# Another order of work in the head of an attention-and-MLP kernel, and two bias vectors computed on VectorE inside the MLP

## The chip, the cores and the metric

The kernel runs on one core of a Trainium2 chip. Its engines have one instruction queue each: TensorE (PE; its weight loads are listed as PEld), VectorE (DVE), ScalarE (ACT), GpSimd (POOL) and SyncE (SP), which here only issues DMAs. ACT and GpSimd issue DMAs as well, from the same queue as their computing instructions. Each engine goes through its queue in order, so an instruction that waits holds up all that stand behind it.

The metric is the device time of one execution in microseconds (us). Before the change it is 2689.59 us, the median of 3 runs (2689.32 to 2691.59).

## What is computed

Two layers on x of shape (2, 512, 32, 32), fp32. Layer 0 is attention with learned sampling positions and a position bias from a small network (its core is below), followed by an MLP. Layer 1 is full attention over the 1024 positions.

```python
# layer 0
xn  = bn(x)
q   = gconv1x1(xn, qw)                                  # 8 groups of 64 channels
off = gelu(depthwise_conv(q, off_dw_w, stride=4) + off_dw_b)
off = tanh(einsum('bchw,oc->bohw', off, off_pw_w)) * 4  # where the 64 keys are sampled
kv  = grid_sample(xn, grid + off)
k, v = gconv1x1(kv, kw), gconv1x1(kv, vw)
pos  = grid_q - grid_kv                                 # (query, key, 2)
bias = sign(pos) * log1p(abs(pos))
bias = relu(bias @ cpb_w1 + cpb_b1)                     # 2 -> 128
bias = relu(bias @ cpb_w2 + cpb_b2)                     # 128 -> 128
bias = bias @ cpb_w3 + cpb_b3                           # 128 -> 1, per query and key
attn = softmax(q k^T * scale + bias)
x = x + out_w (attn v) + out_b
x = x + mlp_w2 gelu(mlp_w1 bn2(x) + mlp_b1) + mlp_b2
# layer 1
q, k, v = x Wq^T + bq, x Wk^T + bk, x Wv^T + bv
x = x + (softmax(q k^T / sqrt(512)) v) Wp^T + bp
```

In layer 1 the kernel multiplies weight matrices with each other beforehand: G = Wq^T Wk for the logits, and the product of Wp and Wv for the output. The biases then shrink to two vectors of 512 numbers, Wk^T bq and Wp bv (+ bp). These two are the "two bias vectors" of the change.

## The kernel before

**Chains.** The 8 pairs of an image and a block of 128 channels (two groups of 64) are worked through in 5 chains: chain 0 and chain 1 with one pair each, chains 2 to 4 with two each. A chain (`chain(ci)`) makes the queries of its pairs (normalise, L260, on ACT; matmuls psq, L266; copies into qa, L271), the depthwise convolution (in chain 0 as 36 taps on VectorE, L303 and L305), gelu (L337), a small matmul po (L345), tanh (L355), and from the positions th the tile ab with sign(pos) * log1p(abs(pos)) for each of 32 coordinates and each key: ab = fe[:, 1], finished by L390. Then ab is written to a scratch tensor in DRAM, fdr, by four DMAs of SP (L392), one for each quarter c of the keys, in runs of 16 floats. `sample(ci)` after it makes the keys and values.

**Main loop.** 256 steps s, each for 4 keys of one group. `load_tables` (L592) loads, every 4 steps, the 16 keys' values back from fdr to all 128 partitions (fb, 512 KB, one buffer, on SP's queue); `st_tables` turns fb into ta (L602) and tb (L607 on VectorE for the first, L609 on ACT for the others). `st_layer1` (L621, VectorE) forms relu(ta + tb) for 4 keys and all queries, h1; `st_layer2` (L638) does 64 passes of TensorE into PSUM; ACT evicts them (L645, L647) into rx, ua or uo, and ub; VectorE adds pairs (L655); and GpSimd's and SP's DMAs add and move parts of the result (a fold, L669; a join, L672 on SP and L674 on GpSimd). A join of one step waits for the fold of the same step. L703 puts the result into the logits. The instructions of chains 1 to 4 are laid between those of the steps as a background program (`later`), one piece per step.

**The head** is everything before the loop's first step. `wake` runs matmuls on zeros (L147). All loads are issued on SP and ACT. `rank()` finds how many of the 128 hidden units have positive last weights and where each goes (two matmuls with one column, L212 and L213, small operations on GpSimd and six on VectorE, L219 to L225); `arrange()` puts the hidden units in that order with matmuls (L229, L232). `weights(0)` and `weights(1)` are the two products of weight matrices (psg, L524, 16 matmuls of two passes each; copied out by ACT, L529, and stored to gdr by GpSimd, L530). `vectors()` computes the two bias vectors with TensorE: 8 matmuls psu (L539), a copy, 8 matmuls put (L548), a copy into ub (L552), and the addition of bp on GpSimd (L553).

Several helpers set the order: `issue_after(x)` places what is recorded inside it behind instruction x in the order in which instructions are laid out; generators (`head`, `g`, `n`, `v`) are advanced by `next`, so that a piece of one is recorded between pieces of another. The tile pools decide by tags and numbers of buffers when a tile may be written again; an instruction that writes a tile waits for its last readers.

**After the loop** comes the projection of layer 0 (L884, L892), in two halves, then the MLP as 8 units (L937), each unit loading its weights on SP, then layer 1's attention (L1056, L1154).

Of the kernel before, what the change touches and what calls it, by code (L numbers as in the profile page):

```python
# [34 lines left out]
    ("bq", 4), ("bv", 4), ("bp", 4), ("dwb", 1), ("cb1", 1), ("cb3", 1),  # L35
# [11 lines left out]
def conv_seq_kernel(ctx: ExitStack, tc: tile.TileContext, x, xt, kst, pst, cst, vec, wsm, outw, w1, w2, wl, out):  # L47
# [16 lines left out]
    for i, g in enumerate(("bn1g", "bn2g")):  # L64
        nc.gpsimd.tensor_scalar(
            bns[:, 4 * i : 4 * i + 4], vs[:, VOFF[g] : VOFF[g] + 4], INV_BN, None, ALU.mult
        )
# [73 lines left out]
    with tc.tile_pool(name="lp", bufs=2) as lp:  # L141
# [20 lines left out]
        nc.gpsimd.memset(prod, 0.0)  # L162
# [12 lines left out]
        nc.scalar.dma_start(out=pz[:, 0:413], in_=pst)  # L175
        nc.scalar.dma_start(out=ws[:, 1024:1408], in_=wsm[:, 1536:1920])
        nc.scalar.dma_start(out=ident, in_=kst)
        nc.scalar.dma_start(out=cs, in_=cst)
# [7 lines left out]
        nc.scalar.dma_start(out=ws[:, P:1024], in_=wsm[:, P:1024])  # L186
# [20 lines left out]
        perm, place = pw_[:, 256:384], pw_[:, 384:512]  # L207
        def rank():
            nc.gpsimd.memset(one, 1.0)
            nc.gpsimd.tensor_scalar(po_, wb[:, 0:1], 0.0, None, ALU.is_ge)  # L210
            ps = flat("rank")
            nc.tensor.matmul(ps[:, 0:1], tri, po_, start=True, stop=True)  # L212
            nc.tensor.matmul(ps[:, 512:513], one, po_, start=True, stop=True)  # L213
            nc.scalar.copy(rn, ps.rearrange("p (h n) -> p h n", h=2)[:, :, 0])
            r_, n_ = rn[:, 0:1], rn[:, 1:2]
            nc.gpsimd.tensor_scalar(pc, chan, n_, r_, ALU.add, ALU.subtract)
            nc.gpsimd.tensor_scalar(dc, pc, r_, po_, ALU.subtract, ALU.mult)
            nc.gpsimd.tensor_tensor(pc, pc, dc, ALU.subtract)
            nc.vector.tensor_scalar(k16, four, n_, 4.0, ALU.is_le, ALU.mult)  # L219
            nc.vector.tensor_reduce(t4, k16, AX.X, ALU.add)  # L220
            free, bound = ([t.rearrange("p (a b l) -> p b a l", a=2, b=2)[:, i] for t in (place, crow)] for i in (0, 1))
            nc.vector.tensor_scalar(bound[0], bound[1], t4, 64.0, ALU.is_ge, ALU.mult)
            nc.vector.tensor_tensor(bound[0], bound[0], bound[1], ALU.add)
            nc.vector.tensor_scalar(free[0], free[1], t4, None, ALU.add)
            nc.vector.tensor_scalar(perm, place, pc, None, ALU.is_equal)  # L225

        def arrange():
            ps = flat("perm")
            nc.tensor.matmul(ps[:, 0:P], w2t, perm, start=True, stop=True)  # L229
            for z in range(4):  # L230
                for u in range(4):
                    nc.tensor.matmul(  # L232
                        ps[32 * u : 32 * u + 32, 512 + 2 * z : 514 + 2 * z], perm[:, 32 * z : 32 * z + 32], wb,
                        start=True, stop=True,
                    )
            nc.scalar.copy(cw2, ps[:, 0:P])
            nc.scalar.copy(
                sc[:, 0:8].rearrange("p (a z) -> p z a", a=2), ps[:, 512:520].rearrange("p (z a) -> p z a", a=2)
            )
            nc.gpsimd.tensor_scalar(sc[:, 8:9], sc[:, 1:2], 0.0, 2.0, ALU.is_ge, ALU.mult)  # L240
            nc.gpsimd.tensor_scalar(sc[:, 8:9], sc[:, 8:9], 1.0, None, ALU.subtract)
            nc.gpsimd.tensor_scalar(sc[:, 0:4], sc[:, 0:4], sc[:, 8:9], None, ALU.mult)
            for z in (1, 3):
                nc.gpsimd.tensor_tensor(sc[:, 4 + z : 5 + z], sc[:, 4 + z : 5 + z], sc[:, z : z + 1], ALU.mult)
            nc.gpsimd.tensor_scalar(w3f[:, 24:32], mask[:, 0:8], sc[:, 8:9], None, ALU.mult)
            nc.gpsimd.tensor_scalar(w3u[:, 28:32], mask[:, 8:12], sc[:, 8:9], None, ALU.mult)

# [3 lines left out]
        def chain(ci):  # L251
# [3 lines left out]
            for i in range(K):  # L255
# [14 lines left out]
                for f_, h_, f, h in QUADS:  # L270
                    nc.scalar.copy(  # L271
                        qa[f_, b, k, h * 512 : (h + 1) * 512], ps[h_, f * 512 : (f + 1) * 512]
                    )
# [67 lines left out]
            ps = flat("po")  # L341
            with tc.issue_after(marks[0]) if ci == 0 else nullcontext():
                for i in range(3):
                    for f in range(2):
                        nc.tensor.matmul(  # L345
                            ps[:, f * 512 + i * n // 2 : f * 512 + (i + 1) * n // 2],
# [7 lines left out]
            for f in range(2):  # L354
                nc.scalar.activation(  # L355
                    th.rearrange("p i (f k) j -> p f i (k j)", f=2)[:, f],
                    ps[:, f * 512 : f * 512 + 3 * n // 2].rearrange("p (i m) -> p i m", i=3), AF.Tanh,
                )
            if ci == 0:

                nc.scalar.activation(hb[:, 9:10], thf[:, 3 * n - 1 : 3 * n], AF.Ln, bias=1.0, scale=0.0)
            if ci > 0:
                yield
            for i in range(3):
                nc.vector.scalar_tensor_tensor(
                    th[:, i], th[:, i], 4.0, jg[:, i].unsqueeze(1).to_broadcast([P, 2 * K, J]),
                    ALU.mult, ALU.add,
                )
            nc.vector.tensor_scalar(thf, thf, 2.0 / 7.0, -1.0, ALU.mult, ALU.add)
# [15 lines left out]
            nc.vector.reciprocal(u, u)  # L385
            nc.vector.tensor_tensor(er, er, u, ALU.mult)
# [4 lines left out]
            for c in range(4):  # L391
                nc.sync.dma_start(  # L392
                    out=fdr[ci][:, c, :, :].rearrange("g p j -> p g j"),
                    in_=ab.rearrange("p (g c j) -> p g c j", c=4, j=KT)[:, :, c, :],
                )
# [111 lines left out]
        with tc.issue_after(nc.cur_bb.bb.instructions[-1]):  # L507
            nc.sync.dma_start(out=wv, in_=wsm[:, 1024:1536])
            nc.sync.dma_start(out=ow_s, in_=outw)
        gs = lp.tile([P, 2, NCH, C], F32, tag="h1", name="gs", bufs=3)  # L510
        bz = ph.tile([P, 2 * NCH, 32], F32, tag="xnt", name="bz")
        nc.gpsimd.memset(bz, 0.0)
        for i, bn in enumerate(("bq", "bv")):
            nc.gpsimd.tensor_copy(
                bz[:, i * NCH : (i + 1) * NCH, 0], vs[:, VOFF[bn] : VOFF[bn] + NCH]
            )

        def weights(i):
            ps = [flat("psg") for _ in range(2)]
            for o in range(NCH):  # L520
                if o == NCH - 1:
                    yield
                for k in range(NCH):
                    nc.tensor.matmul(  # L524
                        ps[k // 2][:, k % 2 * 512 : k % 2 * 512 + 512], wls[i][:, 0, o, k * P : (k + 1) * P],
                        wls[i][:, 1, o, :], start=(o == 0), stop=(o == NCH - 1),
                    )
            for k2 in range(2):
# [4 lines left out]

        def vectors():
            ps = flat("psu")
            rows = ph.tile([P, 2, C], F32, tag="wt", name="rows")
            for i in range(2):
                for o in range(NCH):
                    nc.tensor.matmul(  # L539
                        ps[32 * o : 32 * o + 32, 512 * i : 512 * i + 512], bz[:, i * NCH + o, :],  # L540
                        wls[i][:, 1, o, :], start=True, stop=True,
                    )
            nc.scalar.copy(rows.rearrange("p i c -> p (i c)"), ps)
            yield
            ps = flat("put")
            for i in range(2):
                for k in range(NCH):
                    nc.tensor.matmul(  # L548
                        ps[:, 512 * i + k : 512 * i + k + 1], rows[:, i, k * P : (k + 1) * P], ones,
                        start=True, stop=True,  # L550
                    )
            nc.scalar.copy(ub, ps.rearrange("p (i c) -> p i c", i=2)[:, :, 0:NCH])  # L552
            nc.gpsimd.tensor_tensor(  # L553
                ub[:, 1, :], ub[:, 1, :], vs[:, VOFF["bp"] : VOFF["bp"] + NCH], ALU.add
            )

        def newest(engine):
            return next(i for i in reversed(nc.cur_bb.bb.instructions) if i.engine == engine)

        marks = []  # L560
        head, g, n, v = chain(0), weights(0), weights(1), vectors()
        next(head)
        next(head)
        rank()
        next(head)
        next(g)
        marks.append(newest(mybir.EngineType.PE))
        next(head)

        with tc.issue_after(newest(mybir.EngineType.PE)):  # L570
            next(g, None)
        for _ in head:
            pass
        arrange()
        next(v)
        next(n)
        with tc.issue_after(newest(mybir.EngineType.PE)):
            next(v, None)
# [19 lines left out]
        def st_tables(c):  # L598
# [3 lines left out]
            nc.scalar.activation(  # L602
                ta.rearrange("p j x -> p x j"), fb[:, 0], AF.Identity, bias=col("cb1"), scale=col("w1x")
            )
# [234 lines left out]
    nc.gpsimd.tensor_tensor(uc, ub[:, 0, 0:2], ub[:, 0, 2:4], ALU.add)  # L839
# [16 lines left out]
    with ExitStack() as top, tc.tile_pool(name="wp", bufs=2) as wp:  # L856
# [171 lines left out]
        for i, (b, p) in enumerate(units):  # L1028
            if 0 < i < len(units) - 1:
                load_unit(*units[i + 1])  # L1030
# [5 lines left out]
            layer1(p, wa, xb, hm)  # L1036
            if p == NU - 1 and b == 0:
# [4 lines left out]
            if p == NU - 1 and b == 0:  # L1042
                spread([xb[:, j] for j in range(7)])

# [212 lines left out]
def _layout(np, inputs):  # L1257
# [7 lines left out]
    def twice(v):  # L1265
# [6 lines left out]
        "mb2": cols(L0["mlp_b2"]), "bq": cols(L1["bq"]), "bv": cols(L1["bv"]), "bp": cols(L1["bp"]),  # L1272
# [29 lines left out]
    def quarters(w):  # L1302
# [15 lines left out]
        "wl": wl,  # L1318
    }
# [20 lines left out]
```

## Time and profile before

| | |
|---|---|
| median of 3 runs | 2689.59 us |
| the profiled execution, whole | 2690.77 us |
| its span, first to last instruction | 2688.9 us |
| mean granted TensorE clock | 0.998 |
| TensorE busy | 2664.8 us, 99% |
| VectorE busy | 2244.6 us, 83% |
| ScalarE busy | 1689.0 us, 63% |
| GpSimd busy | 575.3 us, 21% |
| first loop step's matmuls start | 46.61 us |
| first matmul of the MLP starts | 1996.00 us |

A time in the profile is in us from the start of the span. A group's line reads: line, engine, operation, written and read tiles, shapes, how often; then busy time and the mean of one in ns; then the idle time of that engine just before these instructions, and what ended it. In a timeline a line gives the start, the length, and in brackets the idle time before it with what released it. In the chain of waits each piece is what the end depended on at that moment; "SPq" is time in which SP's queue was issuing. A granted clock of 0.50 means that TensorE ran at half speed.

### The profile page before, as it was taken

How to read it: one execution, taken by the hardware profiler on the slowest of the kernel's cores; microseconds unless marked ns; L12 is line 12 of the kernel's file. 1: busy time of each engine (PE TensorE's matmuls, PEld its weight loads, DVE VectorE, ACT ScalarE, POOL GpSimd, SP SyncE). 2: the span in 40 equal slices, each digit the busy share in tenths (PEclk: the TensorE clock that was granted, in tenths of full speed). 3: DMA queues.
4: the chain of work that ended last, by engine and by line, in shares of the span. 5: the costliest groups of instructions: out<-in, count | busy, mean ns of one | idle time of the engine just before them, and what ended most of it. 6: DMA issues, size and time to landing. Idle time of an engine off the chain costs nothing.

```text
span 2688.9 us, 46981 instructions
## 1 busy us (share of the span) xinstructions
PE 2664.8 (99%) x19628; PEld 955.2 (36%) x19628; DVE 2244.6 (83%) x1337; ACT 1689.0 (63%) x2191; POOL 575.3 (21%) x617
## 2 busy tenths in 40 slices
PE   9999999999999999999999999999999999999999
PEld 3323323232333323233333333333344444446455
DVE  5999999999999999999999999999765484466354
ACT  4787798789878788877777777777621131114041
POOL 1222222222222222222222222222243222000000
PEclk9999999999999999999999999999999999999999
DMA  5667776677666676666676776766631110000000
GB/s 186 146 147 148 154 148 138 139 159 154 141 148 144 150 149 145 139 147 142 148 155 138 148 151 145 147 149 142 134 122 47 47 47 32 16 16 0 31 1 31
DMA packets 95219, 314.05 MB, mean 117 GB/s; under 512 B 17184, under 2 KB 19872, under 8 KB 92320
## 3 DMA queue, kind: packets, MB, share of 16 engines
q0 software_dynamic: 57168, 201.88, 40.4%
q1 hardware_dynamic: 36832, 108.02, 11.2%
q8 instruction: 155, 2.54, 0.4%
q10 hardware_dynamic: 1008, 1.15, 0.1%
q14 instruction: 56, 0.46, 0.0%
HBM read 71.67 MB, written 6.55 MB: 29 GB/s over the span
## 4 chain that ended last, share of the span: by engine, by line
PE 85%; DVE 6%; issue 4%; ACT 2%; DMA 2%; SPq 0%; POOL 0%; DVEq 0%; POOLq 0%; ACTq 0%
PE ps L638 54%; PE sw L937 14%; PE sw L1056 9%; DVE h L621 3%; PE sw L1154 2%; PE sim L703 2%; PE psg L524 1%; PE sw L884 1%; DVE ub L655 1%; DMA ua<-uo 1%; DVE uo L655 1%; DMA ua<-ua 0%; ACT prod L313 0%; DVE ua L655 0%; ACT rx L645 0%
## 5 line engine op out<-in xcount | busy, mean ns | idle before, releaser
L638 PE MATMUL ps<-h,cw 128*32 128x512 f32 x16384 | 1786.6, 593 | 12.3 <-ACT rx L645 10.7
L621 DVE CUSTOM_DVE_ANT_1 h<-ta,tb 128x4096 f32<-128x4096 f32 (+1 forms) x257 | 1131.3, 4402 | 47.0 <-PE ps L638 42.0
L638 PEld LDWEIGHTS ps<-h,cw 128*32 128x32 f32 x16384 | 533.9, 110 | 1231.7 <-issue 1151.7
L645 ACT ACTIVATE rx<-ps,sc 128x1024 f32<-128x1024 f32 x512 | 568.3, 1110 | 175.0 <-PE ps L638 165.5
L647 ACT ACTIVATE ub<-ps,sc 128x1024 f32<-128x1024 f32 x256 | 308.0, 1203 | 96.4 <-PE ps L638 96.2
L655 DVE SCALAR_TENSOR_TENSOR ub<-rx,sc,ub 128x1024 f32<-128x1024 f32 x256 | 326.5, 1275 | 5.7 <-ACT ub L647 5.5
L657 POOL DMA_DIRECT2D ua<-ub x128 | 115.1, 899 | 723.6 <-DVE ub L655 692.3
L937 PE MATMUL sw<-xb,w1t 128*128 128x512 f32 x448 | 193.7, 592 | 1.3 <-DVE xs L123 1.3
L657 POOL DMA_DIRECT2D uo<-ub x127 | 119.3, 939 | 348.8 <-DVE ub L655 289.0
L937 PE MATMUL sw<-hm,w2t 128*128 128x512 f32 x448 | 193.6, 592 | 0.0
L647 ACT ACTIVATE ua<-ps,sc 128x1024 f32<-128x1024 f32 x128 | 154.1, 1204 | 58.5 <-PE ps L638 58.3
L674 POOL DMA_DIRECT2D ua<-uo x126 | 109.7, 870 | 365.2 <-DMA ua<-uo 355.5
L647 ACT ACTIVATE uo<-ps,sc 128x1024 f32<-128x1024 f32 x128 | 154.1, 1204 | 42.0 <-PE ps L638 38.8
L655 DVE SCALAR_TENSOR_TENSOR ua<-rx,sc,ua 128x1024 f32<-128x1024 f32 x128 | 163.5, 1277 | 12.5 <-ACT ua L647 12.5
L655 DVE SCALAR_TENSOR_TENSOR uo<-rx,sc,uo 128x1024 f32<-128x1024 f32 x128 | 163.5, 1277 | 11.8 <-ACT uo L647 11.8
L123 DVE TENSOR_TENSOR hm<-hm,sw 128x1024 f32<-128x1024 f32 x56 | 67.5, 1220 | 110.8 <-PE sw L937 110.6
L669 POOL DMA_DIRECT2D ua<-ua x126 | 154.8, 1229 | 2.6 <-DMA ua<-ub 1.5
L937 PEld LDWEIGHTS sw<-xb,w1t 128*128 128x128 f32 x448 | 85.1, 190 | 108.8 <-issue 105.0
L946 ACT ACTIVATE hm<-hm,vs 128x512 f32<-128x512 f32 x64 | 42.6, 714 | 129.0 <-DVE hm L123 129.0
L937 PEld LDWEIGHTS sw<-hm,w2t 128*128 128x128 f32 x448 | 85.2, 190 | 107.1 <-issue 106.4
L123 DVE TENSOR_TENSOR xs<-xs,sw 128x1024 f32<-128x1024 f32 (+1 forms) x48 | 55.5, 1170 | 72.2 <-PE sw L1056 36.0
L1056 PE MATMUL sw<-aT,vt 128*128 128x512 f32 x224 | 96.7, 593 | 0.3 <-ACT aT L1136 0.3
(237 smaller groups left out, 1798.7 us busy)
## 6 DMA issues: line engine op xcount, KB each, us to landing
ua<-ub POOLq DMA_DIRECT2D x128, 512.0 KB, 4.8
uo<-ub POOLq DMA_DIRECT2D x127, 512.0 KB, 5.4
fb<-fdr SPq DMA_DIRECT2D x64, 512.0 KB, 5.1
ua<-ua POOLq DMA_DIRECT2D x126, 256.0 KB, 6.4
ua<-uo SPq DMA_DIRECT2D x126, 256.0 KB, 2.8
ua<-uo POOLq DMA_DIRECT2D x126, 256.0 KB, 3.8
w1t<-in_w SPq DMA_DIRECT2D x8, 1024.0 KB, 4.8
w2t<-in_w SPq DMA_DIRECT2D x8, 1024.0 KB, 4.8
```

Of the source, the lines that this page charges most:

```text
L123: nc.vector.tensor_tensor(out, a, b_, op)
L621: nc.vector._custom_dve(TENSOR_ADD_SAT, out=h1[:, y : y + step].rearrange("p y t x -> p (y t x)"), in0=a.unsqueeze(1).to_broadcast([P, ste ...
L638: nc.tensor.matmul(ps[32 * q : 32 * q + 32, h, :], cw2[:, 32 * z : 32 * z + 32], h1[:, 16 * h : 16 * h + 16, q, :], start=True, stop=True,)
L645: nc.scalar.activation(o, ps, AF.Relu, bias=sc[:, 4 + z : 5 + z])
L647: nc.scalar.activation(o, ps, AF.Relu, bias=sc[:, 4 + z : 5 + z], scale=sc[:, z : z + 1])
L655: nc.vector.scalar_tensor_tensor(r[1], r[0], sc[:, z : z + 1], r[1], ALU.mult, ALU.add)
L657: nc.gpsimd.dma_start(out=sums[s][1], in_=sums[s][3], accum_op=ALU.add)
L669: nc.gpsimd.dma_start(out=lanes(s, 0), in_=lanes(s, 1), accum_op=ALU.add)
L674: nc.gpsimd.dma_start(out=lanes(s, 1), in_=lanes(s + 1, 0), accum_op=ALU.add)
L703: nc.tensor.matmul(sims[gi][q : q + 32, :], w_, t[:, h, :], start=(i == 0 and f == 0), stop=(i == NSL // 4 - 1 and m == len(parts[e]) - 1),)
L937: nc.tensor.matmul(ps[:, m, :], w[:, a, k, m * P : (m + 1) * P], x[:, b_, k, :], start=(k == 0), stop=(k == 1),)
L1056: nc.tensor.matmul(ps[:, m, :], w[:, a, k, c + m * P : c + (m + 1) * P], x[b_][:, k, :], start=(k == 0), stop=(k == nk - 1),)
```

## The change

1. Loads. cs, pz and ident are issued by GpSimd instead of ACT; the later part of ws by SP, behind the output weights, instead of ACT. The scales bns come from VectorE instead of GpSimd. The clearing of prod moves into `arrange()`.
2. Order of TensorE's work. Queries, then 4 products of `weights(0)`, the two ranking matmuls, 9 products, po, the last 3 products, the arranging matmuls, and the 16 products of `weights(1)`. The ranking, po and arranging matmuls of the head write tiles of the `sim` pool. Half of the first chain's copies into qa are done by VectorE.
3. Order of the small work. The VectorE part of the ranking (`order()`) stands behind the taps. The load of the logarithm's table does not read th. For chain 0 the part of th that ab needs is placed first, the rest after the write. The reciprocal writes a tile of its own. The first ta is made in two pieces.
4. The write of ab to fdr is one DMA instead of four, in all chains.
5. `vectors()` is removed. In each of the 8 MLP units SP loads a 128x512 piece of a matrix (wr; and br, one of the biases, spread over all partitions, at two of the units), and VectorE multiplies the two and sums along the row into one column of ub. The two additions that use ub come after the MLP's units.

```diff
-        nc.gpsimd.tensor_scalar(
+        nc.vector.tensor_scalar(
             bns[:, 4 * i : 4 * i + 4], vs[:, VOFF[g] : VOFF[g] + 4], INV_BN, None, ALU.mult
         )
...
-        nc.scalar.dma_start(out=pz[:, 0:413], in_=pst)
         nc.scalar.dma_start(out=ws[:, 1024:1408], in_=wsm[:, 1536:1920])
-        nc.scalar.dma_start(out=ident, in_=kst)
-        nc.scalar.dma_start(out=cs, in_=cst)
+        nc.gpsimd.dma_start(out=cs, in_=cst)
+        nc.gpsimd.dma_start(out=pz[:, 0:413], in_=pst)
+        nc.gpsimd.dma_start(out=ident, in_=kst)
...
-        nc.scalar.dma_start(out=ws[:, P:1024], in_=wsm[:, P:1024])
...
-                    nc.scalar.copy(
-                        qa[f_, b, k, h * 512 : (h + 1) * 512], ps[h_, f * 512 : (f + 1) * 512]
-                    )
+                    copy = nc.vector.tensor_copy if ci == 0 and h == 1 else nc.scalar.copy
+                    copy(qa[f_, b, k, h * 512 : (h + 1) * 512], ps[h_, f * 512 : (f + 1) * 512])
...
-                nc.scalar.activation(hb[:, 9:10], thf[:, 3 * n - 1 : 3 * n], AF.Ln, bias=1.0, scale=0.0)
+                with tc.issue_after(newest(mybir.EngineType.Activation)):
+                    nc.scalar.activation(hb[:, 9:10], ones, AF.Ln)
...
+            place_keys(2 if ci == 0 else 0, 3)
...
-            nc.vector.reciprocal(u, u)
-            nc.vector.tensor_tensor(er, er, u, ALU.mult)
+            rc = acc.rearrange("p a k y x -> p (a k y x)")[0:64, 0:n]
+            nc.vector.reciprocal(rc, u)
+            nc.vector.tensor_tensor(er, er, rc, ALU.mult)
...
-            for c in range(4):
-                nc.sync.dma_start(
-                    out=fdr[ci][:, c, :, :].rearrange("g p j -> p g j"),
-                    in_=ab.rearrange("p (g c j) -> p g c j", c=4, j=KT)[:, :, c, :],
-                )
+            nc.sync.dma_start(
+                out=fdr[ci].rearrange("g c p j -> p (g c) j"), in_=ab.rearrange("p (g j) -> p g j", j=KT)
+            )
+            if ci == 0:
+                place_keys(0, 2)
...
             nc.sync.dma_start(out=ow_s, in_=outw)
+            nc.sync.dma_start(out=ws[:, P:1024], in_=wsm[:, P:1024])
...
-        head, g, n, v = chain(0), weights(0), weights(1), vectors()
+        head, g, n = chain(0), weights(0), weights(1)
         next(head)
         next(head)
-        rank()
+        next(g)
+        with tc.issue_after(newest(PE)):
+            rank()
         next(head)
-        next(g)
-        marks.append(newest(mybir.EngineType.PE))
+        with tc.issue_after(newest(PE)):
+            next(g)
+        marks.append(newest(PE))
         next(head)
-
-        with tc.issue_after(newest(mybir.EngineType.PE)):
-            next(g, None)
+        with tc.issue_after(newest(PE)):
+            next(g)
+        order()
         for _ in head:
             pass
-        arrange()
-        next(v)
-        next(n)
-        with tc.issue_after(newest(mybir.EngineType.PE)):
-            next(v, None)
+        with tc.issue_after(newest(mybir.EngineType.Activation)):
+            next(g, None)
+        with tc.issue_after(newest(PE)):
+            arrange()
+        with tc.issue_after(newest(PE)):
+            next(n)
         next(n, None)
...
-            nc.scalar.activation(
-                ta.rearrange("p j x -> p x j"), fb[:, 0], AF.Identity, bias=col("cb1"), scale=col("w1x")
-            )
+            for j0, j1 in ((0, 4), (4, KT)) if c == 0 else ((0, KT),):
+                nc.scalar.activation(
+                    ta.rearrange("p j x -> p x j")[:, :, j0:j1], fb[:, 0, :, j0:j1], AF.Identity,
+                    bias=col("cb1"), scale=col("w1x"),
+                )
...
         for i, (b, p) in enumerate(units):
+
+            j, k = divmod(i, NCH)
+            if k == 0:
+                br = cp.tile([P, C], F32, tag="kz", name="br")
+                nc.sync.dma_start(out=br, in_=brow[j].partition_broadcast(P))
+            wr = f_pool.tile([P, C], F32, tag="ss", name="wr")
+            nc.sync.dma_start(out=wr, in_=wlt[:, i])
...
             layer1(p, wa, xb, hm)
+            nc.vector.scalar_tensor_tensor(
+                wr, wr, 1.0, br, ALU.mult, ALU.mult, accum_out=ub[:, j, k : k + 1]
+            )
```

## The prediction, made before the changed kernel was run

> **What bounds the kernel now.** The page first. TensorE is busy for the whole span at full granted clock, so outside the head only a hole in the row of matmuls can cost or give time.
>
> ```profile
> span 2688.9 us, 46981 instructions
> PE 2664.8 (99%) x19628; PEld 955.2 (36%) x19628; DVE 2244.6 (83%) x1337; ACT 1689.0 (63%) x2191; POOL 575.3 (21%) x617
> L638 PE MATMUL ps<-h,cw 128*32 128x512 f32 x16384 | 1786.6, 593 | 12.3 <-ACT rx L645 10.7
> ```
>
> Next the list of waits for PE (us in total, times, longest): the rows left out bring the sum to some 20 us. L212 and L266 are the head, L645 is a stall of the loop's evictions, L884 and L937 stand in and after the projection.
>
> ```profile
> PE ps L638 <- ACT rx L645: 10.7, 12, 3.0
> ...
> PE rank L212 <- POOL pwork L210: 1.5, 1, 1.5
> ...
> PE sw L937 <- DVE xs L123: 1.3, 1, 1.3
> PE sw L884 <- DVE xs L123: 1.2, 1, 1.2
> PE psq L266 <- ACT xn L260: 1.0, 1, 1.0
> ```
>
> Then the timeline of PE in the head (start, length), and one row of busy time by stretches (stretch, its length, the five engines' busy time, granted clock, DMA share, GB/s): from 9.45, inside the second hole, the clock is halved for 6.83 us.
>
> ```profile
> 7.56 1.09 PE L266 MATMUL psq<-xn,ws 64*64 64x512 f32 x8 [1.04 <-ACT xn L260]
> 10.17 0.59 PE L212 MATMUL rank<-pwork,pz 128*128 128x1 f32 x2 [1.53 <-POOL pwork L210]
> ...
> 30.89 10.57 PE L524 MATMUL psg<-wl_s 128*128 128x512 f32 x24
> ...
> 46.61 0.64 PE L638 MATMUL ps<-h,cw 128*32 128x512 f32 x4
> ```
>
> ```profile
> 9.45:16.28 6.83, 6.11 (x11) 3.04 (x11) 4.97 (x24) 3.04 (x5) 1.91 (x8) 0.50 1.05 416
> ```
>
> Last, the chain of waits around the largest hole of the loop, 503.47 to 506.47: ab's last operation (L390), four writes of fdr on SP's queue, a join (L672), the load of fb, then ACT's table, for which ACT had waited since 499.6 with evictions behind it.
>
> ```profile
> 492.61 0.42 DVE fe L390
> ...
> 493.04 0.63 SPq L392
> ...
> 497.27 1.77 SPq L392
> ...
> 499.27 0.51 SPq L672
> ...
> 499.89 3.74 DMA fb<-fdr
> ...
> 504.74 0.68 ACT tb L609
> ...
> 506.47 5.75 PE ps L638 x33
> ```
>
> **Head: TensorE's side.** Before, the first loop step starts at 46.61 and ends at 53.68 in the chain of waits. Three things go. (1) The holes of 1.04 and 1.53: xn (L260) started at 6.26, behind ACT's own issues at 4.70, 5.34 and 5.71; now ACT issues three loads early and the scales come from VectorE (vs landed at 4.68, two operations of some 0.2), so xn runs 5.0 to 6.25 under the wake matmuls, which end at 6.51. Queries follow to 7.6 and then four products, no rank: together 2.57. (2) Half clock: 6.11 us of busy time at 0.50 would take half as long, 3.05. (3) The 16 vector matmuls, 1.76 + 1.68 on the chain: 3.44. Sum 9.06. Laid out forwards, with 0.44 per pass (10.57 / 24): queries to 7.6, 8 passes to 11.1, rank 0.5, 18 passes to 19.6, po 0.85 to 20.5, 6 passes to 23.1, perm 0.7, 32 passes to about 37.9. The products' loads are no bound: the slice of each o is in by 6.50, 8.49, 11.90 and 13.26, before its turn.
>
> [...]
>
> **Head: the tables' side.** The taps start after four copies of 2.35 in all, 7.7 + 2.35 = 10.05 instead of 11.10. The copies are now split over ACT and DVE, but the built program's semaphores make each wait for the one before, so nothing is gained there. The six ranking operations (about 1.1 us between the taps) move behind them, so gelu ends near 19.0 and po waits for TensorE's 19.6. From po's end (20.5): tanh 0.6, table load 1.28, 0.15, then Abs at 22.55; Abs to the end of ab took 28.16 to 31.82, 3.66, less 0.85 because the reciprocal no longer waits for Ln to release its tile: 25.4 (before 31.82; the load used to hold the third L365 until 27.13, and two of the three now come later). Write: before, 31.85 to the load's issue at 37.04, 5.2, for the first of four writes; now one write of all 512 runs. Bounds: 4.4 (a little under the median 4.7 of the 20 single writes) and 7.7 (first issue to last landing of the four at chain 2). I take 5.2, as the bytes are few: 30.6. Load 3.33: 33.9. ta's first quarter about 0.5 (between 0.28 for a 128x64 operation and 1.27 for all), both halves of h1 4.5: 38.95. The first four matmuls of the step (8 passes, 1.75) cover 37.9 to 39.6, so this path is just hidden. Step 0 ends at 37.9 + 7.0 = 44.9: **-8.8**. At 4.4 and 0.428 a pass -9.4; at 7.7 h1 ends 41.45, the step 46.7: -7.0.
>
> At no price: the three loads on GpSimd's queue. Each issue takes about 0.9 (the L657 and L674 rows), so they go out by 4.7, and pz is first needed at 11.1; VectorE is idle until then, GpSimd has only memsets, and prod's (1.38) moves to a free stretch. The late part of ws (448 KB) sits behind the output weights on SP, ahead of xnt and xn of chain 1, which nobody waits for before the loop. ACT's gs copies go behind Ln; they only delay buffers needed at 23.
>
> **Loop: the chains' write.** In chains 1 to 4 four issues become one, and the first load must wait for all of it. At chain 2 that meets the stall shown. In the built order the last operation of ab stands behind the 4.41 of layer 1 on VectorE (before: ahead of it, 492.61), and the join of L672 stands ahead of the write on SP. That join waits for a GpSimd fold issued at 490.72 that landed at 497.52 (the page's median for it is 6.4). So the write goes at about 497.7, not 493.04; SP no longer spends 6.0 on four issues. Landing 4.5 to 7.7 (the four together took 7.7, 9.1 and 6.8 in chains 2 to 4), load 3.7: fb at 507.7 against 503.63, **+4.1**. What is late next: ACT's table, the eviction behind it (rx L645), then TensorE, whose PSUM is full. Here nothing else is in front of ACT, so all of it shows, plus 0.3 of half clock (the 3.0 stall was followed by 3.3 us at 0.52): **+4.4**. Lower bound 0.4 (fold lands at once, write as fast as one of the 20, 3 us), upper 8.0. Chains 1, 3 and 4 have their first tables requested later than the write lands in the trace; chain 4's hole (1.94, from sg's wait of 2.4 on the write) may shrink or stay: 0.
>
> **Projection and MLP.** Ten loads and eight VectorE operations on 128x512. Nearest row for one: L892, 0.74 (1.27 for 128x1024 bounds it above). In VectorE's order five of them stand inside the second projection, 1957 to 1996, where VectorE is nearly dense; its pauses there are 0.78 + 1.59 + 0.68 = 3.05. All share one buffer, so each load (256 KB, 2.9 from issue to landing for such a load at 1943.27) starts only when the previous operation is done: I count 1.8 and 0.3 of waits, with the queue behind them (the sums L123 and L892 that TensorE needs). 5 x 0.74 + 2.1 - 3.05 = **+2.7** on the start of the MLP; 0.65 if loads are in time, 5.8 if no pause is used. The other three sit in unit 0, where VectorE pauses some 2 us per product. The two GpSimd sums replace two and feed the last stage only.
>
> **Sum.** -8.8 + 4.4 + 2.7 = -1.7. The profiled execution took 2690.77 (span 2688.9 and 1.9 around it), 1.2 above the median shown: 2690.77 - 1.7 - 1.2 = **2687.9**.
>
> **Rivals.** (A) As summed, 0.50; own range 2684.4 to 2692. (B) The stall of chain 2 does not grow, because fold and write land fast, and the projection costs 1.7, half way between its lower bound and my value: -8.8 + 0.4 + 1.7 = -6.7, 2682.9, faster; 0.30. For it: single writes landed in as little as 2.1, and SP loses 6 us of issuing. Against: the chunks are the same and start later. (C) The write is late for every chain: first tables wait at chains 1, 3 and 4 as at 2, 4.4 each. -8.8 + 4 x 4.4 + 2.7 = +11.5, 2701; it decides from three chains on (+7.1, 2696.7). For it: the same code in all chains. Against: only two waits of ACT for fb stand in the trace, one of them the head's. 0.12. (D) The head gives half, because the clock stays low or the write takes 7.7 and more: -5 + 4.4 + 2.7, 2691.7; 0.08.
>
> **Numbers.** This kernel's runs tell about 0.2% (5.4 us) from no change: faster is under 2684.2, slower over 2695.0. Faster 0.32 (B, a little of A), same 0.54 (A, D), slower 0.14 (C, A's upper bounds). Range: -9.4 + 0.4 + 0.65 gives 2681.2 below; -7.0 + 8.0 + 5.8 would give 2696.4; cut to 2694.5.
>
> **To look for.** The head without a half-clock stretch and with the first L638 near 38; fdr written once, landing within 4.4 to 7.7; a PE hole of some 7 us near 494 to 502, with SP's write behind the join; VectorE's new operation waiting for wr before the MLP. Wrong if the loop's hole is 3 or less (B), if several chains show one (C), or if the head still shows clock 0.5 (D).

## The result, and the profile after

The changed kernel takes 2686.23 us (median of 20 runs, 2684.04 to 2688.40); the kernel before, run beside it, 2690.39 us (20 runs, 2688.26 to 2691.97). The ratio is 0.9987, with a 95% interval of 0.9981 to 0.9993: about 3.5 us faster by the ratio (4.2 between the medians), inside 0.2%. The profiled execution took 2687.88 us with a span of 2686.1 us, 2.8 less than the 2688.9 of before.

Line numbers from here on are those of the changed kernel: L629, L636, L612, L405, L726 and L727 were L638, L645, L621, L390, L735 and L736 before. The page's line for the busiest group, and the list of PE's waits (us in total, times, longest), of the changed kernel:

```profile
L629 PE MATMUL ps<-h,cw 128*32 128x512 f32 x16384 | 1787.8, 593 | 14.2 <-ACT rx L636 13.3
```

```profile
PE ps L629 <- ACT rx L636: 13.3, 11, 5.1
PE sw L927 <- DVE xs L123: 3.0, 1, 3.0
...
PE psq L271 <- ACT xn L265: 0.5, 1, 0.5
PE ps L629 <- DVE h L612: 0.4, 1, 0.4
```

The ranking's wait is gone and the queries' wait is halved, but the longest stall of the loop grew from 3.0 to 5.1 and the wait ahead of the MLP from 1.3 to 3.0. TensorE's holes of the whole trace add up to 21.4 us, 19.5 before; what was gained is the half clock and the removed matmuls in the head. The timeline of PE in the head and one stretch with its clock (the stretch that stood at 0.50 before):

```profile
6.43 1.09 PE L271 MATMUL psq<-xn,ws 64*64 64x512 f32 x8 [0.53 <-ACT xn L265]
...
11.64 7.97 PE L534 MATMUL psg<-wl_s 128*128 128x512 f32 x18
...
37.65 1.07 PE L629 MATMUL ps<-h,cw 128*32 128x512 f32 x8
39.16 6.22 PE L629 MATMUL ps<-h,cw 128*32 128x512 f32 x56 [0.44 <-DVE h L612]
```

```profile
9.45:16.28 6.83, 6.83 (x20) 3.30 (x19) 6.71 (x29) 1.49 (x3) 2.42 (x4) 1.00 1.03 417
```

The first loop step starts at 37.65 and ends at 45.30 (53.68 before). A ledger follows from the start of the same "layer 1" on VectorE in each trace, always minus its start before. By layer 1 the text means `st_layer1`, L612, the first layer of the bias network; there are 257 of these operations in every kernel, numbered from 0:

| layer 1 number (start before) | changed | e_rc | e_best |
|---|---|---|---|
| 4 (58.35) | -8.3 | -8.6 | -8.9 |
| 64 (505.20) | -8.2 | -8.7 | -9.0 |
| 72 (565.81) | -6.4 | -10.5 | -7.9 |
| 96 (745.97) | -6.5 | -10.5 | -7.9 |
| 116 (894.60) | -4.3 | -10.5 | -7.9 |
| 148 (1137.94) | -4.2 | -10.5 | -7.9 |
| 160 (1225.58) | -5.9 | -12.2 | -9.6 |
| 256 (1918.95) | -5.9 | -12.2 | -9.6 |
| end of the span (2688.9) | -2.8 | -10.6 | -10.3 |

Read down the changed kernel's column: 8.3 won in the head, 1.8 lost at chain 2 (64 to 72), 2.2 lost at chain 3 (96 to 116), 1.7 won at chain 4 (148 to 160), 3.1 lost between the loop's end and the MLP. The two losses in the loop look like this. First the chain of waits at chain 2:

```profile
488.54 0.36 SPq L663
...
488.95 3.34 DMA fdr<-fe
...
492.38 5.26 DMA fb<-fdr
...
498.74 0.68 ACT tb L600
...
500.47 1.92 PE ps L629 x5
```

The single write goes out right after the join, lands in 3.34, the load takes 5.26, and TensorE stands for 5.11, up to 500.47. On VectorE the reciprocal now comes three layer 1 operations ahead of ab's last operation L405, and one of them (4.43) directly ahead of it; before, L390 at 492.61 stood ahead of its layer 1:

```profile
466.97 1.76 DVE L400 RECIPROCAL acc<-fe 64x256 f32<-64x256 f32 x1
...
482.89 4.43 DVE L612 CUSTOM_DVE_ANT_1 h<-ta,tb 128x4096 f32<-128x4096 f32 x1
487.23 0.43 DVE L405 SCALAR_TENSOR_TENSOR fe<-fe 64x256 f32<-64x256 f32 x1
```

Then VectorE's timeline at chain 3:

```profile
811.92 0.41 DVE L405 SCALAR_TENSOR_TENSOR fe<-fe 64x256 f32<-64x256 f32 x1
...
814.98 1.20 DVE L726 TENSOR_REDUCE mx<-sx 128x16 f32<-128x1024 f32 x1
816.11 4.40 DVE L612 CUSTOM_DVE_ANT_1 h<-ta,tb 128x4096 f32<-128x4096 f32 x1
820.44 0.16 DVE L727 TENSOR_SCALAR mx<-mx 128x16 f32<-128x16 f32 x1
```

The end of ab and the softmax maximum have slipped together, and a whole layer 1 (4.40) stands between the two operations of the maximum. ACT waited 3.95 for it (0.89 before), with the evictions behind, and TensorE stood 2.33 at 821, followed by 3.41 us at half clock (0.50 from 823.96 to 827.37).

### The profile page after: what moved, and what is told of

It is laid out like the page before. It is cut to its first block, busy times and chain, and to the rows that moved or that the text cites. A ratio compares the mean times of both kernels' runs of the same rounds, so it can differ in the third digit from the quotient of the medians.

```text
span 2686.1 us, 46913 instructions
## 1 busy us (share of the span) xinstructions
PE 2660.2 (99%) x19596; PEld 951.4 (35%) x19596; DVE 2250.8 (84%) x1358; ACT 1687.4 (63%) x2188; POOL 578.3 (22%) x615
## 4 chain that ended last, share of the span: by engine, by line
PE 83%; DVE 7%; issue 5%; DMA 2%; ACT 2%; POOL 0%; SPq 0%; DVEq 0%; POOLq 0%; ACTq 0%
PE ps L629 52%; PE sw L927 14%; PE sw L1058 9%; DVE h L612 3%; PE sw L1156 2%; PE sim L694 2%; DVE ub L646 1%; DMA ua<-uo 1%; PE psg L534 1%; DVE ua L646 1%; ACT prod L317 1%; DVE uo L646 1%; PE sw L874 1%; ACT rx L636 0%; DMA ua<-ua 0%
## 5 line engine op out<-in xcount | busy, mean ns | idle before, releaser
L629 PE MATMUL ps<-h,cw 128*32 128x512 f32 x16384 | 1787.8, 593 | 14.2 <-ACT rx L636 13.3
L612 DVE CUSTOM_DVE_ANT_1 h<-ta,tb 128x4096 f32<-128x4096 f32 (+1 forms) x257 | 1131.7, 4404 | 45.1 <-PE ps L629 41.0
L629 PEld LDWEIGHTS ps<-h,cw 128*32 128x32 f32 x16384 | 533.2, 110 | 1235.4 <-issue 1156.2
L636 ACT ACTIVATE rx<-ps,sc 128x1024 f32<-128x1024 f32 x512 | 569.0, 1111 | 176.4 <-PE ps L629 162.3
L638 ACT ACTIVATE ub<-ps,sc 128x1024 f32<-128x1024 f32 x256 | 308.2, 1204 | 95.9 <-PE ps L629 95.9
L927 PE MATMUL sw<-xb,w1t 128*128 128x512 f32 x448 | 195.1, 596 | 3.0 <-DVE xs L123 3.0
L638 ACT ACTIVATE ua<-ps,sc 128x1024 f32<-128x1024 f32 x128 | 154.2, 1205 | 58.6 <-PE ps L629 58.3
L638 ACT ACTIVATE uo<-ps,sc 128x1024 f32<-128x1024 f32 x128 | 154.1, 1204 | 41.3 <-PE ps L629 39.2
L123 DVE TENSOR_TENSOR hm<-hm,sw 128x1024 f32<-128x1024 f32 x56 | 67.6, 1218 | 106.3 <-PE sw L927 106.0
L123 DVE TENSOR_TENSOR xs<-xs,sw 128x1024 f32<-128x1024 f32 (+1 forms) x48 | 55.6, 1171 | 72.9 <-PE sw L1058 36.0
L592 ACT ACTIVATE ta<-fb,vs 128x512 f32<-128x512 f32 (+1 forms) x65 | 89.4, 1379 | 14.7 <-DMA fb<-fdr 14.7
```

The lines of the kernel that those rows point to most:

```text
L123: nc.vector.tensor_tensor(out, a, b_, op)
L592: nc.scalar.activation(ta.rearrange("p j x -> p x j")[:, :, j0:j1], fb[:, 0, :, j0:j1], AF.Identity, bias=col("cb1"), scale=col("w1x"),)
L612: nc.vector._custom_dve(TENSOR_ADD_SAT, out=h1[:, y : y + step].rearrange("p y t x -> p (y t x)"), in0=a.unsqueeze(1).to_broadcast([P, ste ...
L629: nc.tensor.matmul(ps[32 * q : 32 * q + 32, h, :], cw2[:, 32 * z : 32 * z + 32], h1[:, 16 * h : 16 * h + 16, q, :], start=True, stop=True,)
L636: nc.scalar.activation(o, ps, AF.Relu, bias=sc[:, 4 + z : 5 + z])
L638: nc.scalar.activation(o, ps, AF.Relu, bias=sc[:, 4 + z : 5 + z], scale=sc[:, z : z + 1])
```

## The experiments

All edits are on the changed kernel; each ratio is to the kernel before, with its 95% interval.

### e_rc: the reciprocal in place again in chains 1 to 4

```diff
-            rc = acc.rearrange("p a k y x -> p (a k y x)")[0:64, 0:n]
+            rc = acc.rearrange("p a k y x -> p (a k y x)")[0:64, 0:n] if ci == 0 else u
```

> One edit on the changed kernel: in chains 1 to 4 the reciprocal writes in place again; chain 0 keeps its own tile. Theory: the tile of its own lets the builder place the reciprocal a step earlier on VectorE in chains 2 and 3, which pushes the last operation of ab (chain 2) and the softmax maximum L727 (chain 3) behind a 4.4 us layer 1. Then TensorE's hole of 5.11 at 495 shrinks to at most 1.5, the hole of 2.33 at 821 with its half clock goes, the hole of 1.4 before kv (875 before) may come back: about 4.5 under the changed kernel, 2681.5 (2680 to 2683). Rival, the single write is what makes chain 2 late: the hole at 495 stays near 5, 2685 to 2686.

Measured: 2681.68 us (2680.15 to 2685.00), 0.9969 (0.9957 to 0.9980). The list of PE's waits:

```profile
PE ps L629 <- ACT rx L636: 8.8, 11, 2.9
PE sw L927 <- DVE xs L123: 2.9, 1, 2.9
PE ps L629 <- DVE kv L476: 1.6, 2, 1.4
```

And VectorE's timeline, at chain 2 and at chain 3:

```profile
483.93 0.41 DVE L405 SCALAR_TENSOR_TENSOR fe<-fe 64x256 f32<-64x256 f32 x1
484.26 4.41 DVE L612 CUSTOM_DVE_ANT_1 h<-ta,tb 128x4096 f32<-128x4096 f32 x1
...
813.25 0.15 DVE L727 TENSOR_SCALAR mx<-mx 128x16 f32<-128x16 f32 x1
813.33 4.41 DVE L612 CUSTOM_DVE_ANT_1 h<-ta,tb 128x4096 f32<-128x4096 f32 x1
```

Both operations stand ahead of the layer 1 again. The time is the one expected. The hole at chain 3 is gone and the small one before kv is back, as the theory has it. The hole at chain 2 shrinks to 2.9, the size of before, not to 1.5. In this execution no half clock follows it (granted clock 1.00 from 491.50 to 498.50), which is why the ledger gains 1.8 there instead of losing. The rival falls: the single write is still there. The cause of both losses in the loop is that the reciprocal, no longer held by Ln's reading of its tile, was placed earlier on VectorE, and the operations behind it (L405, and with it the softmax maximum) came to stand behind a layer 1.

### e_four: four writes again in chains 1 to 4

```diff
-            nc.sync.dma_start(
-                out=fdr[ci].rearrange("g c p j -> p (g c) j"), in_=ab.rearrange("p (g j) -> p g j", j=KT)
-            )
+            if ci == 0:
+                nc.sync.dma_start(
+                    out=fdr[ci].rearrange("g c p j -> p (g c) j"), in_=ab.rearrange("p (g j) -> p g j", j=KT)
+                )
+            for c in range(4) if ci > 0 else ():
+                nc.sync.dma_start(
+                    out=fdr[ci][:, c, :, :].rearrange("g p j -> p g j"),
+                    in_=ab.rearrange("p (g c j) -> p g c j", c=4, j=KT)[:, :, c, :],
+                )
```

> One edit on the changed kernel: in chains 1 to 4 four writes of fdr again, as before; chain 0 keeps the single one. Theory (VectorE's order is at fault, not the write): the first of the four starts at 489 as now, SP is held some 6 us by the four issues, the load of fb goes out later than 492.4, the hole at 495 is 5 to 8.5: 2686 to 2689. Rival (the single write, which must land whole, costs the time): the hole falls to 3 or less, 2683.5 to 2684.5.

Measured: 2688.70 us (2687.42 to 2689.80), 0.9995 (0.9986 to 1.0004).

```profile
488.08 0.47 SPq L669 DMA_DIRECT2D ua<-uo  x1
488.59 2.98 SPq L411 DMA_DIRECT2D fdr<-fe  x4
491.69 8.39 SPq L587 DMA_DIRECT2D fb<-fdr  x2
```

This is SP's queue. The hole is 5.2, as with one write, so the rival falls. The theory's detail was wrong too: the four issues held SP 3.0 us, not 6, and the load went out at 491.69, a little before 492.38. The median is 2.5 over the changed kernel; its profile shows one stretch of 3.41 us at half clock more after the hole (1.7 us by estimate, half of 3.41). Whether four writes cost more than that stays open.

### e_late: the bias operations tied to their own MLP unit

```diff
+            on = cp.tile([P, 1], F32, name="on")
+            nc.gpsimd.tensor_scalar(on, hm[:, 0, 0, 0:1], 0.0, 1.0, ALU.mult, ALU.add)
             nc.vector.scalar_tensor_tensor(
-                wr, wr, 1.0, br, ALU.mult, ALU.mult, accum_out=ub[:, j, k : k + 1]
+                wr, wr, on, br, ALU.mult, ALU.mult, accum_out=ub[:, j, k : k + 1]
             )
```

> One edit on the changed kernel: the eight VectorE operations of the bias vectors are tied to their own unit of the MLP by a scale of 1 that GpSimd derives from the unit's hidden values, so that none can stand in the second projection. Theory: the hole of 3.01 before the MLP falls to 1.3 and no half clock follows it: 3.1 less, 2683.1 (2682.5 to 2684). Rival (the loads, or the operations wherever they stand, cost the time): 2685.5 to 2687.

Measured: 2683.47 us (2681.80 to 2685.76), 0.9975 (0.9964 to 0.9985), as the theory has it. VectorE's timeline in the changed kernel, near the end of the projection, and then PE's wait in e_late:

```profile
1966.77 0.68 DVE L1034 SCALAR_TENSOR_TENSOR wr<-wr,br 128x512 f32<-128x512 f32 x1
...
1970.19 0.69 DVE L1034 SCALAR_TENSOR_TENSOR wr<-wr,br 128x512 f32<-128x512 f32 x1 [1.59 <-DMA wr<-in_wlt]
...
1988.07 1.21 DVE L123 TENSOR_TENSOR xs<-xs,sw 128x1024 f32<-128x1024 f32 x1
1989.91 0.69 DVE L1034 SCALAR_TENSOR_TENSOR wr<-wr,br 128x512 f32<-128x512 f32 x1 [0.63 <-DMA wr<-in_wlt]
...
1990.53 1.22 DVE L123 TENSOR_TENSOR xs<-xs,sw 128x1024 f32<-128x1024 f32 x1
```

```profile
PE sw L927 <- DVE xs L123: 1.3, 1, 1.3
```

In the changed kernel the fifth operation waits for its load directly ahead of the last sum L123 that the MLP needs. With the operations in their own units the wait is the 1.3 of before, no half clock stands in the MLP, and the same eight operations and ten loads cost nothing that the time shows.

### e_best: e_rc and e_late together

> The edits of e_rc and e_late together. Theory: both gains add, 2678.5 (2677 to 2680.5), 12 under the kernel before. Rival (either of them is not the cause it is held for): 2681 or more.

Measured: 2678.61 us (2677.08 to 2680.46), 0.9955 (0.9941 to 0.9968). The gains add: 7.6 under the changed kernel, and below both kernels. In the profiled execution the hole of 2.8 at chain 2 was followed by two stretches of 3.41 us at half clock (granted clock 0.86 from 491.50 to 498.30 and 0.63 from there to 505.00), so its ledger loses 1.0 there where e_rc's gained. The two columns of the ledger show single executions: e_rc's profiled one took 2680.15, 1.5 under its median, e_best's 2680.46, 1.9 over its own, so the medians and not the columns compare the two kernels.

### e_rank: ranking ahead of the products

```diff
-        next(g)
+        rank()
         with tc.issue_after(newest(PE)):
-            rank()
+            next(g)
         next(head)
```

> One edit on the changed kernel: the two ranking matmuls stand ahead of the products again, so that TensorE waits for pz (landed 9.29) with 1.1 us of queries done. Theory taken from the row of before (a window of 3.41 us with less than about half of it in use is followed by half clock, with no idle window): a hole of 1.8 and one or two windows at 0.50, the first loop matmul at 41 to 43 instead of 37.65, 2689.5 to 2691.5. [...]

Measured: 2688.85 us (2685.65 to 2692.71), 0.9993 (0.9984 to 1.0003). A miss as a test: in the profiled execution pz landed sooner (8.73) and the wake matmuls ended later (6.89), the hole was 0.67, and no half clock followed; the first loop matmul came at 38.74. It does not test the theory. Its span is 2.2 longer than the changed kernel's; by the ledger 0.7 of that arises in the head and 1.0 at chain 2, where two stretches of 3.41 us at half clock followed the hole instead of one.

### e_act: small loads by ACT again

```diff
+        nc.scalar.dma_start(out=pz[:, 0:413], in_=pst)
         nc.scalar.dma_start(out=ws[:, 1024:1408], in_=wsm[:, 1536:1920])
-        nc.gpsimd.dma_start(out=cs, in_=cst)
-        nc.gpsimd.dma_start(out=pz[:, 0:413], in_=pst)
-        nc.gpsimd.dma_start(out=ident, in_=kst)
+        nc.scalar.dma_start(out=ident, in_=kst)
+        nc.scalar.dma_start(out=cs, in_=cst)
...
+        nc.scalar.dma_start(out=ws[:, P:1024], in_=wsm[:, P:1024])
...
-            nc.sync.dma_start(out=ws[:, P:1024], in_=wsm[:, P:1024])
```

> The small loads are issued by ACT again (cs, pz, ident, the late part of ws), the order of TensorE's work stays the changed one. Theory: ACT's own issues hold xn back to 6.2 to 6.4 again, the hole ahead of the queries grows from 0.5 to about 1.5, the window it lies in stays over half in use, clock 1.00, first loop matmul at 38.7: 2687.3. Rival (this hole alone halves the clock): first loop matmul at 40.4 or later, 2689 or more.

Measured: 2686.86 us (2686.02 to 2689.96), 0.9987 (0.9977 to 0.9996). The hole was 1.13, the first loop matmul came at 38.58, the clock stayed at 1.00, with TensorE busy for 2.28 us of the 3.41 from 6.03 to 9.44: the theory's case. So with ACT issuing these loads the first loop matmul comes 0.9 later, of which 0.4 reaches the ledger (7.9 instead of 8.3). In the time nothing of it can be told from noise: the ratio is that of the changed kernel.

### e_both: both delays of the head together

```diff
-            nc.gpsimd.tensor_scalar(po_, wb[:, 0:1], 0.0, None, ALU.is_ge)
+            nc.gpsimd.tensor_scalar(dc, hb[:, 0:1], 0.0, None, ALU.mult)
+            nc.gpsimd.tensor_scalar(po_, wb[:, 0:1], dc, None, ALU.is_ge)
```

besides the edits of e_rank and e_act.

> Both head delays of before together in the changed kernel: ACT issues the small loads (as in e_act), the ranking matmuls stand ahead of the products (as in e_rank), and their input waits for hb, so for cs, as it did before. Theory (two holes in one window of 3.41 us leave it less than half used, and that halves the clock, with no idle window): holes of about 1.1 and 1.3, one or two windows at 0.50 in the head, first loop matmul at 42 to 43.6, 2690 to 2692.5. Rival (holes of this size do not lower the clock; the half clock of before had another cause): clock 1.00 to the loop, first loop matmul near 40.2, 2688.5 to 2689.5.

Measured: 2691.44 us (2687.85 to 2693.49), 1.0002 (0.9992 to 1.0012). Three stretches of 3.41 us of e_both (after the length: PE, PEld, DVE, ACT and POOL busy, then the granted clock):

```profile
4.63:8.04 3.41, 1.67 (x7) 0.32 (x9) 0.24 (x2) 1.24 (x1) 0.00 (x0) 1.00 1.06 390
8.04:11.46 3.42, 2.01 (x14) 0.94 (x7) 1.17 (x4) 1.30 (x3) 1.14 (x4) 1.00 1.05 389
11.46:14.87 3.41, 3.41 (x5) 1.35 (x4) 3.35 (x14) 1.30 (x2) 0.58 (x2) 0.50 1.06 429
```

The holes were 1.74 and 1.42, and 3.41 us at 0.50 followed; the first loop matmul came at 41.68, a little before the range given. The rival falls, by the time and by this execution: putting the delays back brings half clock back. The theory's limit, less than about half of 3.41 us in use, was an estimate from before, where TensorE was busy for 1.60 us from 6.00 to 9.41, ahead of 6.83 us at 0.50. No run shows such a limit: here the 1.67 us in use from 4.63 to 8.04 were followed by 1.00, and the 2.01 from 8.04 to 11.46 by 0.50. The head's ledger gains 4.9 instead of 8.3, so the holes and the 3.41 us at half clock cost 3.3 there; the median lies 5.2 over the changed kernel's, and the other 2 are not seen in this execution.

### e_vec and e_vecrc: the vectors on TensorE in the head

`vectors()` is put back as it was, with its 8 matmuls psu ahead of the last 16 products and 8 put behind them, and the MLP's loads and operations are removed. e_vecrc adds e_rc's edit.

> The bias vectors by 16 matmuls in the head again, the VectorE operations and loads of the MLP left out. Theory: the head 3.1 longer (3.44 less the hole of 0.44 that the tables leave), first loop matmul at 41.1; the MLP starts 3.1 sooner (hole 1.3, no half clock): 2686.2 within 1. Rival (the tables' path would have set the head's end without them too): first loop matmuls end as in the changed kernel, 2683.

Measured: 2690.12 us (2689.29 to 2690.57), 0.9998 (0.9989 to 1.0008), 4 over the expectation. The head did as expected: the first loop matmul at 41.23, the ledger's gain 5.4 instead of 8.3, so the vectors cost 2.9 there. The MLP's wait was 1.3. But the hole at chain 2 was 6.9, followed by two stretches of 3.41 us at half clock: the fold that the join waits for landed 6.94 after its issue (5.98 in the changed kernel) and the write took 5.33 instead of 3.34. By the ledger chain 2 costs 2.2 more than in the changed kernel.

> e_vec with the reciprocal in place in chains 1 to 4, as in e_rc: vectors on TensorE in the head, VectorE's order in chains 2 and 3 as before. It differs from e_best only in where the bias vectors are made. Theory: first loop matmul at 41.2, hole at chain 2 near 2.9, MLP hole 1.3: 2681.8 (2680.5 to 2683), so making the vectors in the MLP at the right place is worth about 3. Rival (e_vec's hole of 6.9 at chain 2 comes from the vectors' matmuls, not from the order): hole near 5 or more, 2684 or more.

Measured: 2685.15 us (2681.80 to 2687.21), 0.9977 (0.9968 to 0.9987). The first loop matmul at 40.65 and the MLP's wait of 1.3 are as expected, but the hole at chain 2 is 3.8, between the two cases: here the write, issued early at 487.04, took 7.6 to land, and two stretches of 3.41 us at half clock followed (granted clock 0.88 from 490 to 503 and 0.74 from there to 510). With VectorE's order of before the hole falls from 6.9 to 3.8; that it is not 2.9 goes with the write, which was issued 12.2 us ahead of layer 1 number 64 as in e_best, but took 2.3 longer. The median is 6.5 over e_best. The spans of the profiled executions differ by 5.0: 2.9 in the head, 0.8 at chain 2, 0.3 in the rest of the loop and 1.0 behind it, where TensorE waited 1.43 in the projection instead of 0.60. The other 1.5 between the medians is not assigned.

### e_early: chain 2 a step earlier

```diff
             nc.scalar.activation(ab, pos, AF.Abs)
-            if ci > 0:
+            if ci > 0 and ci != 2:
                 yield
```

on e_best.

> e_best, and chain 2 does Abs and the addition after it in one step instead of two, so that all that follows in the background stands a step (some 7 us) earlier. Theory: fb of chain 2 lands before ACT comes to its table, the hole of 2.8 at 494 and the half clock after it go: 3 to 6 under e_best, 2674.5 (2672.5 to 2676.5). Rival (the stall moves on: the softmax maximum near step 72 now has a layer 1 between its two operations): 2677.5 to 2681.

Measured: 2678.65 us (2677.05 to 2680.43), 0.9954 (0.9938 to 0.9969), the same as e_best. The list of PE's waits:

```profile
PE ps L629 <- DVE kv L476: 4.9, 3, 2.8
PE ps L629 <- ACT rx L636: 4.2, 7, 1.0
```

The profiled execution took 2677.05. The hole at chain 2 did go, as the theory has it, but the stall moved on, as the rival has it, though to another place: the keys' operation L476 now stands behind a layer 1 at 535 (1.72) and 856 (2.83).

## Why the prediction was right, step by step

The sign and the range held, and so did a change inside 0.2%; the sum of -1.7 was -2.8 in the profile and about -3.5 by the ratio. That the sum came so near is partly luck. Chain 2 was put 2.6 too dear and the start of the MLP 1.0, and a gain of 1.7 at chain 4 was left out; against that the head gave 0.5 less, and losses of 2.2 at chain 3 and 1.4 of half clock in the MLP were left out.

- **Head, -8.8: -8.3.** First loop matmul 37.65 (37.9 worked out), write issued 25.23 (25.4), load issued 30.23 (30.6), fb landed 33.88 (33.9), step 0 ended 45.30 (44.9). The tables' path was to be just hidden and was just not: 0.44 of waiting. The three parts are shown apart: 2.9 for the vectors (e_vec), 3.3 for holes and 3.41 us at half clock (e_both), and before had 6.83 us of it, by estimate 1.7 more (half of 3.41): 7.9 of the 8.3 together. The product's loads were to be no bound; one held TensorE 0.26. The queries' wait was to go wholly, and 0.53 of it stayed: the wake matmuls ended at 5.89, not 6.51, and xn at 6.38.
- **The half clock in the head.** It was put down to the holes, and e_both bears it out: with holes of 1.74 and 1.42 it came back, 3.41 us at 0.50. What decides whether half clock follows a hole is not shown.
- **Loop, chain 2, +4.4: +1.8.** The mechanism and the order were right (ab's last operation behind layer 1, the join ahead of the write, issued at 488.95, which is 497.2 in the times of before, against 497.7). Mis-sized were the write, 3.34 where 4.5 to 7.7 was given (from the four writes of before), and the load, 5.26 where 3.7 was. The 0.3 for half clock cannot be a fixed price: none followed the hole of 2.9 in e_rc, and two stretches of 3.41 us the hole of 2.8 in e_best (last section). The prediction did not say which edit makes the order; e_rc shows the reciprocal's own tile, which it counted only as a gain.
- **Loop, "Chains 1, 3 and 4 have their first tables requested later than the write lands": wrong in its conclusion.** The sentence is true, and asked only after the tables. The same edit moved the softmax maximum behind a layer 1 at chain 3, +2.2; e_rc takes it away.
- **Chain 4, 0: -1.7.** Its hole of 1.94 is gone. It was to go by the single write or stay; in e_four, with four writes, the ledger gains the same 1.7 there, so the number of writes is not the cause. The traces show what the hole hung on. The tile sg (L413, L428 in the changed kernel) takes fe's buffer, so ACT's first operation on it waits for the write that reads fe. Before, that write stood behind a join that went out at 1144.24, 1.6 after ab was done, and ACT waited 2.40 for it. In the changed kernel and in e_four the join was out 1.7 to 2.0 ahead of ab's last operation, and ACT did not wait. In e_vecrc the join went out 1.5 after ab, and ACT waited 1.10. Why the join comes earlier is not shown.
- **Projection, +2.7: +3.1.** Five operations of 0.69 + 0.08 stood where they were expected, the waits for loads were 1.59 and 0.63 (1.8 and 0.3 expected), but the hole ahead of the MLP grew from 1.31 to 3.01: its start moved by 1.7, not 2.7. Left out was the half clock after it, about 1.4: the MLP's first group rose from 193.7 to 195.1. The sum comes near because the two errors cancel. e_late shows that the place is the cause and not the work.

Of the rivals, (B) gave the size of the stall's growth better than the forecast (0.4 and 4.4 given, 1.8 measured), (C) had one thing right, that more than one chain pays, though by another mechanism.

## What to carry to other kernels

When an edit frees an instruction from a wait, look where the builder then puts it and what is pushed behind the long instructions of that engine, in every stage that shares the code: a gain put at 0.85 us in one chain (from Abs to the end of ab the head took 2.8 instead of 3.66) was paid for with two stalls in others. Extra work "in the idle time of an engine" must be tied to that idle time by a dependence, or it may stand where its inputs are ready first: here five of eight operations stood in the densest stretch. A stage-by-stage ledger of one repeated instruction shows such gains and losses that cancel in the total.

## What the runs showed of the hardware

- A hole costs what it lasts, and half clock can come on top: at 0.50 the median matmul of L524 in the kernel before took 1.06 us (starts from 11.0 to 15.5), at 1.00 0.59 (16.7 to 23.6). In the changed kernel the holes of 5.11 (chain 2), 2.33 (chain 3) and 3.01 (ahead of the MLP) were each followed by 3.41 us at 0.50; in the kernel before, the 3.0 at chain 2 by 3.41 us, the 1.04 and 1.53 in the head by 6.83 us. At chain 2 a hole of 2.9 was followed by no half clock in e_rc, and one of 2.8 by two stretches of 3.41 us in e_best. Around the hole TensorE was busy for 2.35 and 1.60 us in two stretches of 3.41 in e_rc; in e_best for 1.38 us in the 3.41 ahead of 0.50 (e_rc, then e_best):

```profile
492.44:495.85 3.41, 2.35 (x24) 0.52 (x16) 3.41 (x2) 1.00 (x1) 2.59 (x3) 1.00 0.63 160
495.85:499.26 3.41, 1.60 (x16) 0.55 (x20) 3.41 (x2) 3.41 (x5) 0.05 (x1) 1.00 1.04 190
...
493.05:496.46 3.41, 1.38 (x16) 0.17 (x8) 3.41 (x3) 2.02 (x3) 2.36 (x3) 1.00 0.80 168
496.46:499.87 3.41, 2.61 (x16) 0.65 (x20) 3.41 (x1) 3.38 (x5) 0.00 (x0) 0.50 1.07 169
```

- The busy time of such a stretch alone does not tell whether half clock follows: the 1.60 us of before (6.00 to 9.41) and the 2.01 of e_both (0.6 of it one-column matmuls) were followed by half clock, the 1.67 of e_both and the 1.60 of e_rc were not. What decides is not shown.
- The first six matmuls on zeros took 4.15 us in the profiled execution of e_early and 5.33 in those of e_rank and e_vec. The queries behind them wait for xn as well, so with the changed loads they began between 6.29 (e_vecrc) and 6.82 (e_rank, e_vec): this moves the head by some 0.5 us from run to run.
- The single write of ab, 1024 runs of 64 bytes, took 2.55 us to land at chain 3 of the changed kernel. At chain 2 it took 2.66 to 3.45 in five of the six kernels in which it went out behind the join (changed, e_late, e_rank, e_act, e_both), 5.33 in the sixth (e_vec), and 5.33 to 7.59 in the four in which it went out ahead of the join (e_best, e_rc, e_early, e_vecrc). What sets the time is not shown.
